# New places for the operations at both ends of a software-pipelined graph-network kernel, written in the order of their places

## Chip, cores and metric

The kernel runs on one core of a Trainium2 chip. The time is device microseconds of one execution; of several runs the median is taken. TensorE (PE) does the matrix products, VectorE (DVE) and ScalarE (ACT) read and write PSUM banks and SBUF, GpSimd (POOL) works on SBUF, and the queue of SyncE (SP) issues the transfers. Each engine runs its own instructions in order and waits on semaphores for the others.

## What is computed

64 graphs of 256 nodes with 512 features pass two layers, all in float32. For each graph:

```python
# layer 0
h   = maximum(layernorm(x), 0)
agg = (adj @ h) / maximum(adj.sum(-1), EPS)
x   = x + relu(concatenate([h, agg]) @ W.T)
# layer 1
h   = maximum(layernorm(x), 0)
Xw  = h @ Wv + bv
e   = leaky_relu(sj[None, :] + si[:, None] + ab, 0.2)   # sj, si: Xw times the halves of aw
T   = adj * exp(e);  T = T / T.sum(-1)
H, Xk = 0, h
for k in range(3):
    H  = H + Xk @ Wk[k] + bk[k]
    Xk = T @ Xk
x   = x + relu(H)
```

## The kernel before

**Products.** The matrix products are written in forms with fewer multiplications (seven products in place of eight for 2 x 2 blocks, and a larger form for x·W in `wide`). Their sums and differences run on DVE, POOL and ACT, and most matmuls take a 128x128 block against a 128x256 block. The matmul line is L459 for all of them. PSUM has eight banks of 128x512.

**Stages.** A graph goes through a list of stages. `loads` fetches x and adj; `prepare` makes the first norm and relu (`norm_relu`, L347), scales the adjacency by the degree (`scaled`, L567), and transposes both; `prepared` ends this; `wide` is h times the weights of layer 0, `layer0` the adjacency times that and the residual (`finish`, L563). `turn1` is the second norm, then four multiplications with sums on DVE (L677) that give sj and si. `transition` builds T: ds (L686) writes sj to DRAM, row (L687) reads it back to all partitions, ACT makes the leaky relu (L692) and the exponential (L695), DVE multiplies by adj and sums (L697), ACT scales (L703). `moved` and `once` form T·h, `inner` the inner hop, `turned1` reads the transposed h back, and `outer` makes the products with Wk that end in the output. Work on a graph is spread over several turns: loads go three graphs ahead, `prepare` and `prepared` one ahead, `moved` to `outer` one behind.

**Transposing.** Most graphs transpose through DRAM: DVE turns blocks (L376), SP writes them (`dh`, `dan`, `dtt`, L380) and reads them back (L386). The first graphs and the last two use PE for some of it instead (`flip_on_pe`: matmul against the identity at L404, copied out at L408 to L410).

**Order.** Nothing in the code's own sequence sets the order on an engine. Every operation is put into a `Plan` (`add`) with its engine, a cost (which the program passes to a `note` that does nothing), and the keys that it reads and writes. Its place is a number: the entry of the table `AT` for its stage and its count in that stage, plus graph number times TURN (38.52), plus a shift for graphs near the end. `emit` sorts each engine's operations by place, and each engine runs that list. Tables named for a stage alone hold for the middle graphs; `_0`, `_1`, `_2` hold for the first three, `_last` and `_late` for graphs 63 and 62, and `first` and `weights` for the loads of the first inputs and the preparation of the weights. `emit` goes round the engines and writes, for each, every operation whose forerunners are written; the framework sets semaphores in that sequence.

**First inputs.** SP's first loads are the halves of graph 0's x, the four parts of W (L787 on), adj of graph 0 and 1, x of graph 1, the halves of Wv and the blocks of Wk. PE transposes the parts of W (L796) and of Wv (L848), and DVE makes the sums of W's form.

**The last product.** `main` (L527) makes the seven products of a 2 x 2 form, numbered by `step`, in PSUM. `p`, `r` and `d` are its three banks; `plus` (L474) adds a known term to the product in bank p and puts it into the bank where a later product is then accumulated: its seed. In the last graph two more banks, x and y, are given, so that each quarter of the output can leave as soon as it is ready (`last`, L756: relu and residual on DVE, then a DMA of the quarter). There the seed for product 3 goes first into the upper half of bank r; after product 2, which accumulates in the lower half of bank r, ACT copies it to bank y (L546), where product 3 accumulates:

```python
plus(bank[r][:, hi], [f"bank{r}"], p, lo, s12, keys[1:])
...
step(2, r, lo, terms)
add("ACT", 0.37, lambda: nc.scalar.copy(bank[y][:, lo], bank[r][:, hi]), [f"bank{r}"], [f"bank{y}"])
last(0, lo, r, lo)
step(3, y, lo, terms)
last(0, hi, y, lo)
```

Of the kernel before, what the change touches and what calls it, by code (L numbers as in the profile page):

```python
# [11 lines left out]
AF = mybir.ActivationFunctionType  # L12
# [15 lines left out]
    "first": (-90.93, -53.23, -117.99, -108.94, -110.36, -116.23, -69.23, -51.75, -160.39, -107.21, -61.21, -22.37, -27.53, -12.34, -45.26, -1.78,  # L28
        -84.29, -28.27, -93.32, 13.37, -47.15, -20.43, -156.60, -71.50, -119.21, -46.84, -42.27, -129.45, -122.63, -61.71, -52.35, -32.94, -72.67,
        -62.56, -45.91, -151.57, -67.52, -60.72, 2.83, 15.02, -11.78, 19.40, 29.16, -47.95, -25.77, 48.23, -47.81, -32.81, -19.46, -48.89, 7.13,  # L30
        20.41, -32.63, 17.85, 10.53, -123.51, 5.76, 21.86),
    "inner": (105.13, 108.59, 106.23, 109.69, 109.89, 110.76, 112.05, 116.38, 111.97, 114.07, 117.47, 117.50, 122.79, 115.08, 117.06, 118.02, 137.51),
    "inner_0": (104.64, 107.10, 112.63, 109.63, 108.85, 109.21, 114.17, 115.99, 113.73, 110.41, 129.80, 114.72, 119.54, 110.75, 113.34, 116.02,
        129.11),
    "inner_1": (110.70, 112.22, 111.49, 112.47, 113.83, 115.31, 114.08, 115.66, 116.33, 115.18, 129.29, 117.74, 125.91, 116.89, 117.80, 117.56,
        155.03),
    "inner_2": (110.70, 111.20, 111.98, 113.63, 111.78, 114.32, 114.94, 116.88, 115.46, 116.06, 116.42, 116.98, 124.86, 117.74, 119.04, 117.57,
        134.35),
    "inner_last": (336.53, 367.29, 384.59, 334.45, 391.73, 454.67, 522.64, 533.37, 408.60, 470.37, 504.02, 528.93, 492.30, 558.54, 500.07, 537.12,
        580.23),  # L40
    "inner_late": (108.31, 111.76, 110.85, 113.85, 112.13, 112.69, 114.05, 114.68, 123.33, 115.61, 145.82, 118.27, 122.89, 115.88, 119.11, 120.04,
        164.89),
    "layer0": (20.96, 24.01, 34.26, 38.15, 36.30, 37.47, 38.90, 39.56, 40.20, 40.90, 41.49, 42.16, 41.93, 42.79, 43.22, 43.47, 44.25),
    "layer0_0": (43.30, 43.73, 40.76, 63.15, 62.04, 64.91, 63.69, 65.17, 65.45, 66.86, 68.03, 68.37, 68.31, 69.19, 69.32, 68.45, 68.75),
    "layer0_1": (31.27, 36.57, 33.97, 43.43, 46.13, 48.74, 46.62, 49.21, 46.86, 49.66, 48.01, 49.83, 48.25, 48.79, 50.67, 49.93, 50.78),
    "layer0_2": (24.88, 28.19, 23.22, 43.47, 37.98, 37.09, 39.47, 39.22, 40.19, 41.59, 40.57, 42.04, 42.75, 43.10, 41.23, 47.00, 44.33),
    "layer0_last": (50.01, 57.68, 33.91, 60.79, 65.66, 66.71, 68.41, 66.94, 69.01, 68.24, 69.91, 69.27, 70.80, 71.03, 72.73, 71.96, 75.23),
    "layer0_late": (15.20, 21.71, 35.30, 40.31, 42.84, 48.47, 47.89, 49.57, 47.98, 49.76, 48.90, 49.94, 48.91, 50.48, 49.70, 51.70, 50.97),
    "loads": (-59.49, -45.29),
    "loads_2": (-40.12, -36.06),  # L50
    "loads_last": (-58.91, -32.90),
    "loads_late": (-54.89, -85.13),
    "moved": (89.04, 92.46, 93.17, 93.66, 94.15, 98.50),
    "moved_0": (94.08, 96.00, 97.15, 96.58),
    "moved_1": (87.63, 93.34, 94.62, 96.56, 97.69, 105.10),
    "moved_2": (88.68, 91.56, 91.23, 91.84, 96.02, 106.19),
    "moved_last": (139.05, 163.46, 205.96, 169.91),
    "moved_late": (96.66, 97.72, 100.63, 101.15),
    "once": (61.25, 64.00, 75.09, 75.88, 94.29, 95.59, 94.96, 99.41, 98.19, 98.63, 100.80, 101.23, 101.56, 100.30, 105.75, 103.00, 102.97, 103.89,
        106.56, 107.35, 108.14),  # L60
    "once_0": (85.34, 86.38, 98.69, 87.50, 93.62, 98.46, 98.58, 97.73, 98.58, 100.34, 100.69, 102.20, 101.36, 98.56, 103.24, 103.33, 102.27, 102.98,
        104.33, 105.25, 108.42),
    "once_1": (57.59, 69.48, 97.24, 96.50, 95.31, 95.58, 95.01, 99.66, 97.26, 98.27, 100.29, 102.15, 100.46, 102.80, 103.34, 105.40, 106.15, 108.95,
        105.21, 110.88, 111.17),
    "once_2": (63.41, 76.25, 69.81, 96.68, 93.52, 97.13, 93.09, 100.30, 100.95, 102.43, 103.05, 103.30, 102.21, 102.90, 103.59, 109.13, 104.57,
        107.39, 107.54, 109.97, 115.46),
    "once_last": (102.80, 135.83, 148.28, 162.89, 124.41, 120.18, 145.98, 187.50, 162.35, 203.89, 212.10, 233.57, 187.89, 213.05, 223.02, 232.11,
        256.18, 243.42, 255.25, 267.18, 321.27),
    "once_late": (66.99, 88.23, 64.29, 90.92, 99.96, 101.37, 100.45, 101.19, 101.37, 101.90, 105.80, 107.13, 110.31, 103.81, 110.60, 107.37, 105.93,
        106.50, 106.70, 107.63, 115.35),  # L70
    "outer": (108.93, 110.52, 122.87, 129.37, 114.22, 117.68, 119.41, 120.07, 120.70, 121.57, 122.87, 123.53, 124.60, 125.46, 126.33, 126.99, 127.62,
        130.65, 131.52, 132.19, 128.92, 131.95, 134.55, 134.99, 141.93, 152.31, 138.02, 140.19, 162.69, 160.60, 164.14, 164.93),
    "outer_0": (94.35, 98.74, 125.62, 106.70, 102.31, 116.27, 117.12, 118.24, 117.50, 117.80, 121.31, 124.46, 124.00, 125.58, 126.52, 126.71, 128.22,
        128.87, 132.65, 133.67, 128.80, 131.21, 134.36, 137.61, 140.55, 144.44, 136.33, 141.49, 160.49, 160.36, 163.66, 166.03),
    "outer_1": (106.89, 111.90, 118.77, 120.53, 108.75, 117.68, 119.18, 119.21, 120.59, 120.95, 123.23, 122.93, 123.75, 126.63, 126.70, 127.43,
        127.87, 128.74, 130.19, 132.33, 130.44, 131.84, 139.05, 141.13, 148.79, 152.10, 133.45, 136.68, 160.29, 160.80, 164.22, 166.72),
    "outer_2": (108.39, 111.96, 127.91, 140.81, 108.40, 121.23, 123.19, 121.63, 124.71, 125.64, 126.27, 125.65, 128.28, 128.68, 129.01, 128.91,
        131.04, 134.92, 135.36, 134.36, 132.23, 135.69, 137.94, 142.17, 143.69, 152.32, 138.41, 140.22, 150.30, 161.80, 164.00, 171.57),
    "outer_last": (498.02, 668.57, 694.33, 671.17, 577.46, 581.61, 593.26, 565.87, 615.19, 623.17, 650.49, 630.60, 695.13, 726.44, 735.87, 784.68,
        743.01, 838.42, 843.34, 796.04, 842.17, 761.60, 792.50, 751.08, 788.70, 811.00, 818.37, 858.45, 840.44, 876.17, 953.80, 975.74, 975.14,  # L80
        1020.56, 876.63, 891.60, 907.44, 875.80, 872.80),
    "outer_late": (109.06, 117.31, 186.73, 151.51, 116.15, 116.30, 119.62, 120.47, 120.01, 120.90, 123.12, 123.38, 129.10, 132.52, 132.66, 129.78,
        134.77, 139.77, 140.44, 139.50, 141.87, 144.49, 145.13, 158.57, 188.07, 200.85, 150.49, 152.04, 158.47, 232.29, 199.18, 211.96),
    "prepare": (-43.06, -41.74, -40.72, -35.30, -36.24, -28.72, -27.19, -23.45, -19.80, -15.93, -24.36, -24.98, -20.94, -12.75, -1.76, -2.28, -14.82,
        -13.49, -12.68, -12.13, -11.03, -11.58, -0.32, 1.04, 0.48, 2.14, 1.59),
    "prepare_0": (-84.88, -53.30, -37.93, -28.72, -22.39, -78.13, -74.85, -6.63, -18.20, -7.49, -144.71, -60.68, -137.04, -101.76, -12.58, -21.22,
        -26.38, -2.11, -10.47, 18.05),
    "prepare_1": (-15.07, -17.62, -8.06, -6.13, -0.14, -1.19, -0.63, 0.54, 7.75, 18.63, -38.44, -18.61, -14.54, 4.73, 16.46, 7.28, 12.55, 17.02,
        21.02, 19.33),
    "prepare_2": (-29.75, -29.48, -28.24, -24.75, -27.62, -28.40, -18.19, -16.40, -14.88, -13.91, -13.33, -6.35, -3.17, 8.62, 7.51, 7.67, -7.58,  # L90
        -2.32, -3.08, -1.25, 10.97, -0.12, 9.45, 9.24, 6.13),
    "prepare_last": (-41.49, -47.42, -40.82, -36.74, -38.40, -39.37, -36.21, -27.41, -24.96, -22.93, -7.95, -5.29, -3.53, 0.52, -2.38, -0.41, -8.95,
        -8.06, 0.10, 9.16, 6.05, -3.83, 2.64, 1.68, 2.00, -1.88, -3.02),
    "prepare_late": (-34.61, -47.32, -24.01, -19.75, -22.44, -22.19, -20.22, -19.93, -12.10, -16.22, -28.31, -35.76, -26.99, -25.62, -0.63, -19.64,
        -11.10, -13.45, -13.43, -9.03, -11.19, -7.53, -0.35, -0.68, -1.43, -1.97, 0.33),
    "prepared": (-7.18, 5.89, 11.28),
    "prepared_0": (8.94, 11.22, 28.01, 44.28),
    "prepared_1": (30.89, 31.47, 31.46, 30.86),
    "prepared_2": (13.00, 25.59),
    "prepared_last": (9.25, 6.90, 2.69),  # L100
    "prepared_late": (-3.13, 0.63, 10.23),
    "transition": (52.39, 56.28, 64.51, 63.42, 65.05, 63.97, 66.52, 67.12, 67.73, 68.04, 68.40, 68.92, 69.51, 71.25, 71.80, 70.70, 72.35),
    "transition_0": (74.09, 74.94, 85.61, 86.74, 87.55, 87.22, 90.49, 90.24, 90.60, 91.41, 91.25, 92.03, 91.61, 91.53, 93.51, 94.10),
# [6 lines left out]
    "turn1_1": (49.63, 49.70, 50.51, 51.10, 51.13, 51.73, 53.03, 53.21, 53.66, 53.93, 58.29, 58.86, 64.81, 54.56, 54.30, 58.29, 62.00, 58.02, 61.54),  # L110
    "turn1_2": (43.11, 45.01, 43.93, 52.82, 53.16, 53.50, 49.16, 51.40, 52.03, 52.20, 54.30, 57.90, 58.08, 51.29, 54.09, 59.58, 56.28, 52.52, 56.97),
    "turn1_last": (75.41, 78.96, 77.17, 178.47, 184.64, 192.21, 86.15, 103.27, 80.59, 81.84, 83.21, 85.38, 104.79, 93.44, 122.16, 115.84, 150.29,
        115.69, 113.30),
    "turn1_late": (42.12, 48.32, 51.63, 53.75, 53.93, 54.07, 55.81, 56.33, 52.09, 61.66, 67.71, 71.29, 74.60, 66.82, 79.34, 84.95, 89.16, 79.81,
        97.48),
    "turned1": (100.59,),
# [859 lines left out]
```

## Time and profile before

| | us |
|---|---|
| median of 3 runs | 2546.91 (2546.01 to 2550.6) |
| profiled execution, its time | 2545.75 |
| its span | 2544.0 |
| PE busy | 2509.1 (99%) |
| DVE, POOL, ACT busy | 1653.6, 1560.1, 1322.6 |
| granted TensorE clock, mean | 0.997 |

The span runs from the first to the last instruction, and the execution's own time is 1.75 us longer. The page's second part shows the span in 40 slices of 63.6 us. The busiest groups are the products of L459, with 380 ns for a matmul alone and 1.03 us for four back to back. A bracket at the end of a row, such as [2.09 <-ACT bank L546], is the idle time of that engine before the row and what ended it.

### The profile page before, as it was taken

The page shows a single profiled execution, that of the slowest core. Times are in us where ns is not written, and L with a number is a line of the kernel's source. Part 1 is how long each engine was busy: PE and PEld are TensorE (multiplying, and loading weights), DVE is VectorE, ACT ScalarE, POOL GpSimd, SP SyncE. Part 2 cuts the span into 40 slices and gives each one's busy share as a digit, 9 for nine tenths or more (in the row PEclk, how much of TensorE's full clock was granted, in tenths as well). Part 3 has the DMA queues.
Part 4 walks back from the last instruction along what each step waited for, and adds up shares of the span by engine and source line. Part 5 has one row for each costly group of instructions (what it writes and reads, how often), then busy time and mean ns, then how long its engine had stood idle before and what let it go on. Part 6 is the DMA issues. An engine that isn't in the chain of part 4 may idle for free.

```text
span 2544.0 us, 39950 instructions
## 1 busy us (share of the span) xinstructions
PE 2509.1 (99%) x12412; PEld 2213.5 (87%) x12412; DVE 1653.6 (65%) x4099; ACT 1322.6 (52%) x3551; POOL 1560.1 (61%) x2475
## 2 busy tenths in 40 slices
PE   7899999999999999999999999999999999999998
PEld 5688888888888888888888888888888888888887
DVE  5766666666666666666666666666666666666654
ACT  7455555555555555555555555555555555555521
POOL 5565666666666666666666656656666666666640
PEclk9999999999999999999999999999999999999999
DMA  4354454454454454444444544544544544544421
GB/s 150 85 131 117 113 129 120 115 125 117 117 129 112 115 135 110 119 125 120 120 120 116 127 121 111 128 122 113 127 119 117 126 113 116 135 112 115 110 71 44
DMA packets 574571, 296.85 MB, mean 117 GB/s; under 512 B 417171, under 2 KB 540819, under 8 KB 574358
## 3 DMA queue, kind: packets, MB, share of 16 engines
q1 hardware_dynamic: 574358, 294.31, 47.0%
q8 instruction: 98, 1.61, 0.3%
q14 instruction: 115, 0.94, 0.1%
HBM read 162.80 MB, written 131.40 MB: 116 GB/s over the span
## 4 chain that ended last, share of the span: by engine, by line
PE 96%; DVE 1%; DMA 1%; SPq 0%; ACT 0%; issue 0%; POOL 0%; DVEq 0%; ACTq 0%; POOLq 0%
PE bank L459 96%; DMA dh<-turned 0%; DMA x<-in_L_gnn_W_dram 0%; DMA l<-in_L_gnn_Wv_dram 0%; SPq L380 0%; DVE bank L474 0%; DVE zg L420 0%; DMA out_dram<-x 0%; DVE z L677 0%; DVE turned L376 0%; PE bank L404 0%; ACT h1n L362 0%; DVE bank L652 0%; SPq L345 0%; DVE zg L474 0%
## 5 line engine op out<-in xcount | busy, mean ns | idle before, releaser
L459 PE MATMUL bank<-l,s 128*128 128x256 f32 x3292 | 876.9, 380 | 6.6 <-ACT bank L546 2.1
L459 PEld LDWEIGHTS bank<-l,s 128*128 128x128 f32 x3292 | 611.6, 191 | 91.4 <-issue 5.1
L471 ACT COPY stg<-bank 128x256 f32<-128x256 f32 x944 | 337.2, 371 | 524.8 <-PE bank L459 203.6
L459 PE MATMUL bank<-l,zg 128*128 128x256 f32 x1820 | 469.2, 380 | 1.6 <-ACT mz L471 0.9
L459 PE MATMUL bank<-lq,zg 128*128 128x256 f32 x1792 | 447.8, 380 | 3.7 <-DVE zg L474 1.3
L459 PEld LDWEIGHTS bank<-lq,zg 128*128 128x128 f32 x1792 | 340.4, 190 | 51.1 <-DVE zg L474 2.3
L459 PEld LDWEIGHTS bank<-l,zg 128*128 128x128 f32 x1820 | 337.2, 191 | 42.3 <-ACT mz L471 1.7
L422 POOL TENSOR_TENSOR zg<-zg 128x256 f32<-128x256 f32 x183 | 131.7, 733 | 353.8 <-ACT zg L471 347.4
L652 DVE TENSOR_TENSOR bank<-bank,stg 128x256 f32<-128x256 f32 x505 | 210.3, 428 | 202.1 <-PE bank L459 138.8
L459 PE MATMUL bank<-l,h0t 128*128 128x256 f32 x1008 | 291.3, 382 | 1.6 <-DVE q L652 0.8
L422 POOL TENSOR_TENSOR s<-h0t,s 128x256 f32<-128x256 f32 x315 | 234.0, 743 | 0.5
L459 PEld LDWEIGHTS bank<-l,h0t 128*128 128x128 f32 x1008 | 197.4, 197 | 26.8 <-DVE q L652 2.3
L677 DVE SCALAR_TENSOR_TENSOR z<-h1n,v_sb 128x512 f32<-128x512 f32 x256 | 211.9, 828 | 13.1 <-ACT h1n L368 4.4
L459 PE MATMUL bank<-l,h1t 128*128 128x256 f32 x784 | 203.3, 381 | 1.3 <-DVE lo L477 1.0
L471 ACT COPY qf<-bank 128x256 f32<-128x256 f32 x128 | 47.6, 372 | 285.3 <-DVE qf L474 250.3
L422 POOL TENSOR_TENSOR qf<-qf 128x256 f32<-128x256 f32 x122 | 113.5, 930 | 117.4 <-DVE qf L474 117.4
L459 PEld LDWEIGHTS bank<-l,h1t 128*128 128x128 f32 x784 | 153.1, 197 | 20.1 <-DVE lo L477 2.3
L563 DVE SCALAR_TENSOR_TENSOR x<-bank,x 128x512 f32<-128x512 f32 x254 | 165.4, 686 | 2.7 <-PE bank L459 1.9
L459 PE MATMUL bank<-q,sa 128*128 128x256 f32 x512 | 152.9, 380 | 2.3 <-DVE bank L474 1.6
L459 PE MATMUL bank<-qf,st 128*128 128x256 f32 x512 | 152.6, 380 | 0.8 <-DVE qf L420 0.7
L422 POOL TENSOR_TENSOR s<-h0t 128x256 f32<-128x256 f32 x189 | 143.5, 773 | 9.3 <-ACT h0t L410 6.6
L422 POOL TENSOR_TENSOR hf<-h1n,hf 128x256 f32<-128x256 f32 x124 | 91.3, 736 | 89.9 <-PE bank L459 89.9
(178 smaller groups left out, 4418.3 us busy)
## 6 DMA issues: line engine op xcount, KB each, us to landing
dh<-turned SPq DMA_DIRECT2D x500, 128.0 KB, 3.3
h1t<-dh SPq DMA_DIRECT2D x64, 512.0 KB, 3.8
x<-in_x_dram SPq DMA_DIRECT2D x63, 512.0 KB, 4.6
out_dram<-x SPq DMA_DIRECT2D x63, 512.0 KB, 3.1
h0t<-dh SPq DMA_DIRECT2D x61, 512.0 KB, 4.0
a<-in_adj_dram SPq DMA_DIRECT2D x64, 256.0 KB, 4.3
dan<-turneda SPq DMA_DIRECT2D x248, 64.0 KB, 1.9
raw<-dan SPq DMA_DIRECT2D x62, 256.0 KB, 2.7
```

The lines of the kernel that those rows point to most:

```text
L422: add("POOL", cost, lambda: getattr(nc.gpsimd, f)(to, p, q), reads, writes)
L459: nc.tensor.matmul(ps, lhs, rhs, start=start, stop=True, skip_group_check=True)
L471: add("ACT", 0.37, lambda: nc.scalar.copy(dst, bank[b][:, cols]), [f"bank{b}"], dkeys)
L563: add("DVE", 0.75 if sums else 0.69, lambda c=c: nc.vector.scalar_tensor_tensor(t[:, c, :], bank[banks[1 + c]], 0.0, t[:, c, :], op0=ALU.m ...
L652: add("DVE", 0.43, lambda f=f, to=to, x=x, y=y: getattr(nc.vector, f)(to, x, y), pbk + [k], tok)
L677: add("DVE", 0.79, lambda s=s, c=c: nc.vector.scalar_tensor_tensor(scr.rearrange("p c n -> p (c n)"), h[:, c, :], 1.0, v_sb[:, s, :], op0= ...
```

## The change

The text of the change has four parts.

1. New numbers in `AT` for `first`, `weights`, and for all tables `_0`, `_1`, `_2`, `_last` and `_late`. Of the tables for the middle graphs only one number of `inner` differs, 117.47 to 117.62. Which operations there are stays the same, apart from part 4.
2. `emit` writes one operation at a time, the one with the lowest place among the engines' next operations that are ready, in place of a run of ready operations for one engine after another.
3. Three of the costs on ACT operations with sums are set higher.
4. In `main`, for the last graph, the seed of product 3 goes to the lower half of its own bank; ACT's copy is left out.

```diff
 AT = {
-    "first": (-90.93, -53.23, -117.99, -108.94, ...
+    "first": (-259.48, -286.32, -474.02, -306.06, ...
...
-    "transition_0": (74.09, 74.94, 85.61, 86.74, 87.55, 87.22, 90.49, ...
+    "transition_0": (61.61, 65.18, 81.16, 82.84, 81.31, 85.36, 81.78, ...
...
@@ emit
-            for e, queue in queues.items():
-                while heads[e] < len(queue) and self.ops[queue[heads[e]]][2] <= done:
-                    i = queue[heads[e]]
-                    self.ops[i][1]()
-                    done.add(i)
-                    heads[e] += 1
-                    left -= 1
+            ready = [(self.ops[q[heads[e]]][3], e) for e, q in queues.items() if heads[e] < len(q) and self.ops[q[heads[e]]][2] <= done]
+            if ready:
+                e = min(ready)[1]
+                i = queues[e][heads[e]]
+                self.ops[i][1]()
+                done.add(i)
+                heads[e] += 1
+                left -= 1
@@ norm_relu
-                add("ACT", 0.66, lambda c=c: nc.scalar.activation(h[:, c, :], s[:, c, :], AF.Identity, ...
+                add("ACT", 0.82, lambda c=c: nc.scalar.activation(h[:, c, :], s[:, c, :], AF.Identity, ...
...
@@ main
         p, r, d = banks[:3]
+        e, cols = (banks[4], lo) if last else (r, hi)
...
-        plus(bank[r][:, hi], [f"bank{r}"], p, lo, s12, keys[1:])
+        plus(bank[e][:, cols], [f"bank{e}"], p, lo, s12, keys[1:])
         step(7, p, lo, terms)
         if last:
-            x, y = banks[3:]
+            x = banks[3]
...
             step(2, r, lo, terms)
-            add("ACT", 0.37, lambda: nc.scalar.copy(bank[y][:, lo], bank[r][:, hi]), [f"bank{r}"], [f"bank{y}"])
             last(0, lo, r, lo)
-            step(3, y, lo, terms)
-            last(0, hi, y, lo)
+            step(3, e, cols, terms)
+            last(0, hi, e, cols)
```

Read off the two built programs, the engines' orders differ in about the first four graphs and the last three; between them each engine has the same instructions in the same order. On SP, the 512 KB of graph 1's x now come first, then the parts of W with the halves of graph 0's x between them, and graph 0's adj after W, which before came second. On PE, one group of four transposes of W and the first two products of graph 0's `wide` stand between and behind the two flips of its h, ahead of the first transposes of Wv. In `transition` of graph 0, ds and row follow one another on SP; on ACT the degree sums of graph 2 stand outside that stage; on DVE the two operations of L697 stand between the additions of graph 1's `layer0`; the two of L703 are neighbours on ACT.

## Prediction

> **What bounds the kernel now.** I began with the page's first two parts and the chain that ended last.
>
> ```profile
> PE 2509.1 (99%) x12412; PEld 2213.5 (87%) x12412; DVE 1653.6 (65%) x4099; ACT 1322.6 (52%) x3551; POOL 1560.1 (61%) x2475
> ...
> PE   7899999999999999999999999999999999999998
> ...
> PEclk9999999999999999999999999999999999999999
> ...
> PE 96%; DVE 1%; DMA 1%; SPq 0%; ACT 0%; issue 0%; POOL 0%; DVEq 0%; ACTq 0%; POOLq 0%
> ```
>
> TensorE does everything that counts. It idles 2544.0 − 2509.1 = 34.9 us in the whole span, and the slices put this into the first and last of them. The change keeps TensorE's number of instructions and, from graph 3 to graph 61, every engine's order. So only the ends are at stake, and I cut them into windows (columns: length, PE, PEld, DVE, ACT and POOL busy, granted clock, DMA share, GB/s).
>
> ```profile
> 0.00:20.00 20.00, 9.95 (x45) 8.29 (x46) 7.35 (x23) 12.97 (x37) 3.13 (x14) 1.00 0.95 314
> 20.00:40.00 20.00, 19.90 (x84) 12.42 (x83) 13.26 (x25) 16.37 (x44) 15.39 (x19) 0.92 0.50 160
> 40.00:60.00 20.00, 17.54 (x85) 12.53 (x85) 13.78 (x36) 13.79 (x39) 11.84 (x18) 1.00 0.01 1
> 60.00:80.00 20.00, 14.65 (x59) 9.89 (x57) 14.15 (x35) 13.05 (x38) 15.70 (x25) 0.95 0.33 60
> 80.00:100.00 20.00, 15.23 (x66) 11.79 (x65) 14.34 (x38) 9.10 (x25) 9.74 (x13) 0.80 0.48 112
> 100.00:120.00 20.00, 18.07 (x81) 14.60 (x80) 13.56 (x28) 6.98 (x22) 11.27 (x18) 1.00 0.34 80
> 120.00:140.00 20.00, 20.00 (x108) 18.09 (x107) 14.04 (x38) 12.03 (x33) 9.99 (x17) 1.00 0.53 125
> ```
>
> Length less PE busy is the idle time: 10.05, 0.10, 2.46, 5.35, 4.77, 1.93 and 0.00. So 24.7 of the 34.9 us are lost before 120 us, 14.6 of them after the first 20. Busy time hides a second loss: the clock is halved in three stretches, 19.9 to 23.35, 77.96 to 88.20 and 2535.55 to 2538.97. In the second PE is busy 6.52 us at clock 0.50, which costs 3.3 more; in the first and the third, 3.4 us each, 1.7. The time at stake is thus 24.7 + 5.0 at the start, and at the end 2.1 + 1.7 (below).
>
> **The parts of the change, one by one.**
>
> *Writing in order of place.* Each engine's queue is sorted as before; only the sequence in which the queues are written differs. It adds no instruction. Where two engines only read one bank, it can turn round which of them waits. In the steady part no engine's order changes: 0. The three cost notes are not used in the program: 0.
>
> *First 24 us: loads and weights.* SP now issues graph 1's 512 KB of x before W, and graph 0's 256 KB of adj after W. The transfers land in order of issue: the four 512 KB parts of W at 4.2, 7.1, 9.0 and 11.0, with 256 KB of adj or x ahead of each but the first, which from 7 us on is about 1.35 us for 512 KB and 0.7 for 256. PE starts on W's first pair at 7.14. With x1 and x0 instead of adj ahead of it I estimate 7.1 + 1.3 = 8.4, and for the second pair, with 256 KB more ahead, 11.7 instead of 11.0: +0.7 at the point where PE has both. In return four transposes of W and two first products of graph 0's `wide` now stand between and behind the flips of its h, ahead of the first transposes of Wv. They fill the waits from 15.4 to 19.6 us, which in the trace are 0.23, 0.79 and the 1.22 for Wv: −2.2. Net **−1.5**. If the half clock behind them stays away too, −3.2; if the loads are late and nothing is filled, +0.7.
>
> *24 to 115 us: graph 0's chain.* The stalls are those of one chain through graph 0: turn1, transition, flip on PE, once, inner. The rows around it:
>
> ```profile
> 57.78 0.35 SPq L686 DMA_DIRECT2D ds<-sj  x1
> 63.50 0.35 SPq L380 DMA_DIRECT2D dh<-turned  x1
> 63.94 0.44 SPq L687 DMA_DIRECT2D row<-ds  x1
> ```
>
> ds had landed at 61.8, but its reader stands behind a dh write that waited for data: 2.1 us of hold. The row lands at 67.3 and ACT comes to it at 68.77, after two scalings of graph 2's adjacency: 1.5.
>
> ```profile
> 69.86 0.72 ACT L695 ACTIVATE z<-z 128x256 f32<-128x256 f32 x2
> ...
> 76.99 0.49 ACT L703 ACTIVATE an<-z,tot 128x256 f32<-128x256 f32 x1
> 77.65 1.52 ACT L368 ACTIVATE h1n<-x,nmr,rstd 128x512 f32<-128x512 f32 x2 [0.17 <-POOL nmr L366]
> 79.08 0.49 ACT L703 ACTIVATE an<-z,tot 128x256 f32<-128x256 f32 x1
> ```
>
> The exponentials end at 70.6, yet their first reader on DVE (L697) runs at 74.41, since it stands behind graph 1's two finishing operations (73.16 and 73.79), which wait for PE: 3.8. The second half of the scaled transition follows the first by 2.1 us instead of 0.5, because a norm of graph 1 lies between: 1.6. After the change ds and row are issued one behind the other, graph 2's adjacency no longer lies on ACT between them, L697 stands between the additions of graph 1's layer0, and the two L703 are neighbours. What SP moves back for it, the dh writes of graph 0's normed rows, is written from 63.50 to 74.4 and read back only at 81.64 (SP's rows), so the slip of some us finds 7 us of room. So the first flip can come 2.1 + 1.5 + 3.8 = 7.4 us earlier (77.5 → about 70), and the second 9.0. PE sees it here:
>
> ```profile
> 77.53 0.44 PE L404 MATMUL bank<-ident,an 128*128 128x128 f32 x2 [0.74 <-ACT an L703]
> 79.62 0.69 PE L404 MATMUL bank<-ident,an 128*128 128x128 f32 x2 [1.65 <-ACT an L703]
> ...
> 85.31 1.19 PE L459 MATMUL bank<-l,s 128*128 128x256 f32 x2 [1.61 <-ACT stg L471]
> ```
>
> Not all of it becomes time: PE's queue is in order, and graph 1's layer0 and graph 2's product stand around the flip. At stake are 14.6 of idle and 3.3 of half clock, 17.9. I went through the new order by hand, every operation at the duration of its row (pair of 128x256 products 0.51 to 0.59, ACT copy 0.37, DVE sum 0.42, POOL sum 0.74, a write and a read back through DRAM 5 to 7): PE has the work that it had done at 115 us done 17.8 us earlier, 1.8 of them from the first part, 16.0 from this one. The walk gives each hand-over nothing (the trace has 0.05 to 0.1), doesn't see POOL and DVE queue for each other, and each of these puts some of the stalls back one step later: late next are graph 0's two products of once (94.00, behind DVE) and h0t of graph 3 from SP (issued 100.34). I take two thirds of the 17.9: **−11.5**, about 4 of it before 75 us. Ends: −16.0 (the walk) and 0 (graph 0 is bound by its DRAM round trips and another wait takes each place).
>
> POOL gets no additional operations. DVE and ACT carry the same work in less time; at 14 of 20 us busy DVE is the fullest, and this is why I don't take the walk.
>
> *The last product.* Before, product 3's seed lay in the upper half of the bank that product 2 writes, and ACT copied it out (L546):
>
> ```profile
> 2532.44 0.76 DVE L474 TENSOR_TENSOR bank<-bank,lo 128x256 f32<-128x256 f32 x2 [4.74 <-PE bank L459]
> 2533.24 0.75 DVE L756 SCALAR_TENSOR_TENSOR x<-bank,x 128x256 f32<-128x256 f32 x2
> ...
> 2534.08 0.36 ACT L546 COPY bank<-bank 128x256 f32<-128x256 f32 x1 [13.70 <-DVE x L756]
> 2534.49 1.13 PE L459 MATMUL bank<-l,s 128*128 128x256 f32 x4 [2.09 <-ACT bank L546]
> 2535.46 1.82 PE L459 MATMUL bank<-l,h1t 128*128 128x256 f32 x4
> ```
>
> PE waits 2.09 us for a copy that itself sits behind DVE's two output operations on the same bank. After the change DVE writes the seed directly into its own bank, product 3 long has it, and PE's new order puts products with 2.2 us of work after product 7, more than the 1.2 that DVE needs for the two seeds. The stall goes: −2.1. What is late next is DVE's last output and the DMA, as before. Two rows before and one after show what the stall brings along: four products take 1.82 us instead of 1.03, and this lasts 3.4 us: −1.7. The Trainium skill, "TensorE: Matmul & The Clock Gate", section "HAM oscillation — how this bites in real kernels", has "no PE-idle gaps >~3.4µs" as the rule; by it a gap of 2.09 would not bring the half clock, it would be there for other reasons and stay: −2.1 alone. The trace shows full clock and no gap over 1 us in the 5 us before it; I take the row, **−3.8**. The same page, section "Part 1: The HAM clock gate (the "warmup" mystery)", says the window runs freely and that the place of the change differs from run to run. This speaks against counting on the clock at the start, hence the two thirds.
>
> *Other places of the last two graphs.* The last graph's other stalls, 0.8, 0.85, 0.84 and 0.85, keep their causes. Graph 62's outer loses a cover (+0.45), the last layer0 gains one (−0.5): 0, ends −2 and +2, the 3 us that graph 62 stalls now.
>
> **Sum**: −1.5 − 11.5 − 3.8 = −16.8 from the profiled execution's 2545.75 gives 2528.95. The median of the three runs lies 1.16 above the profiled one, so 2530.1: **2530 us**.
>
> **Rivals.** *A. Full walk*: start −17.8, end −3.8: 2525; speaks for it that the holds are plainly other work in line; against, a full DVE. *B. Half the start*, −6.5, and the end: 2537. *C. Only the end*: 2543; for it, 7.4 us of holds are less than the round trips of the chain (57.8 to 67.3 for ds and row alone), against it, those 7.4 are visible. *D. Slower*: ACT is in order, and its Prelu (L692) on the row now stands earlier, in front of the copies that free PE's banks. Before, the row was there 1.5 us before ACT was. If in the first graphs SP or the v products are late and the row isn't there, ACT stands, and PE runs dry behind it: 3 to 5 us in each of three graphs, +9 to +15 with the end's −3.8, some 2553. It decides as soon as the row lands over 4 us after ACT has come to it. *E. It doesn't do what it says*: if the writing order alone is in force, no order of an engine changes and the time is 2547; but the orders do differ in the first four graphs.
>
> **Numbers.** Measured differences below 0.2% (5.1 us) can't be told from none. Chances: forecast (2526 to 2534) 0.40, A 0.20, B 0.20, C 0.10, D 0.07, E 0.03. The range 2520 to 2542 leaves out D, E and half of C at the top, and a walk with the clock's gain and the late graphs' −2 at the bottom. Faster (below 2541.8): the forecast, A, B and some of C, 0.87; same 0.06, slower 0.07.
>
> **What would show it.** In the changed kernel's windows: idle before 120 us near 13 instead of 24.7, clock 1.00 from 60 to 100; the first flip of graph 0 near 70 us, ds and row issued within 5 us, L697 within 1 us of the exponentials; no L546, no gap over 1 us in the last 12 us of PE, clock 1.00 there. I am wrong if PE's idle moves to 100 to 140 us, if ACT idles on row for more than 2 us, or if half clock turns up in new places.

## The result, and the profile after

| | before | after |
|---|---|---|
| median of 6 runs, us | 2548.26 (2546.01 to 2550.6) | 2535.84 (2534.51 to 2536.98) |
| ratio, 95% interval | | 0.9951 [0.9939, 0.9964] |
| profiled execution: time, span, us | 2545.75, 2544.0 | 2535.3, 2533.5 |
| PE busy, idle within the span, us | 2509.1, 34.9 | 2501.0, 32.5 |

The change makes the kernel 12.4 us faster by the medians and 10.5 by the two profiled executions, where 16.8 were forecast; 2530 was predicted, with 2520 to 2542 as the range. Here is the windows view of the changed kernel, with the columns as before (length, PE, PEld, DVE, ACT, POOL busy, granted clock, DMA share, GB/s).

```profile
0.00:20.00 20.00, 7.31 (x39) 6.28 (x40) 6.10 (x20) 10.81 (x30) 2.04 (x11) 0.95 0.91 330
20.00:40.00 20.00, 19.69 (x84) 11.85 (x83) 11.05 (x26) 16.14 (x47) 14.64 (x20) 0.88 0.45 131
40.00:60.00 20.00, 19.08 (x93) 14.53 (x93) 14.27 (x38) 14.99 (x41) 12.31 (x18) 1.00 0.01 1
60.00:80.00 20.00, 15.62 (x68) 10.89 (x67) 16.72 (x47) 15.54 (x47) 14.97 (x25) 1.00 0.29 57
80.00:100.00 20.00, 17.32 (x86) 13.87 (x85) 14.56 (x42) 10.75 (x32) 12.36 (x16) 1.00 0.73 172
100.00:120.00 20.00, 18.05 (x81) 14.89 (x81) 12.08 (x30) 8.09 (x23) 9.97 (x18) 1.00 0.33 77
120.00:140.00 20.00, 20.00 (x106) 18.04 (x107) 11.99 (x32) 11.22 (x31) 16.45 (x24) 1.00 0.57 138
```

PE's idle time fell by only 2.4 us and its busy time by 8.1: most of what was gained is time in which PE counts as busy and its matmuls are slow, not gaps. Three things stand out in the windows. The half clock from 78 to 88 us is gone (1.00 from 40 us on), though the one at the start now lasts from 17.9 to 24.7 us instead of 19.9 to 23.3. The idle time from 20 to 120 us fell from 14.6 to 10.2 us. But the first 20 us idle 12.7 instead of 10.05, and the clock from 20 to 40 is 0.88 instead of 0.92: at the start, where 1.5 us had been forecast as a gain, the windows show none.

Windows of equal time hold unequal work, so I used a second account. The 6256 products and transposes that PE has to do need 2483.3 us at full clock (0.433 us for a product of 128x128 by 128x256, 0.108 for a transposed block, as in the rows of the middle). At each point in this work, the time at which the trace shows it done, less the work so far, is what PE has lost: idle, half clock and slow first matmuls together. PE's order is different at the ends, but the work done is comparable. The losses in us at five points, for all kernels of this study:

| kernel | 10 us of work | 30 | 110 (about 150 us) | 2360 | 2474 | end |
|---|---|---|---|---|---|---|
| before | 17.35 | 20.04 | 43.46 | 43.88 | 52.65 | 57.52 |
| after | 18.61 | 21.22 | 36.61 | 36.19 | 46.04 | 46.86 |
| 1 seed alone | 18.01 | 20.70 | 43.94 | 44.04 | 52.81 | 53.64 |
| 2 new start alone | 15.99 | 18.60 | 32.82 | 54.20 | 63.86 | 64.69 |
| 3 new ends and seed | 18.91 | 21.60 | 44.79 | 46.56 | 56.45 | 57.28 |
| 4 new writing alone | 18.27 | 20.96 | 42.87 | 64.51 | 73.28 | 74.11 |
| 5 writing and one number | 17.28 | 19.97 | 41.70 | 42.42 | 50.39 | 51.22 |
| 6 after, flips moved | 19.61 | 22.22 | 37.35 | 37.48 | 47.34 | 48.16 |
| 7 after, x1 later | 18.90 | 21.51 | 36.48 | 36.39 | 46.16 | 46.99 |
| 8 after, old ends | 18.04 | 20.65 | 35.75 | 36.16 | 44.12 | 44.95 |
| 9 after, old ends, mixed writing to 0 | 16.86 | 19.46 | 34.43 | 33.67 | 41.64 | 42.46 |
| 10 the same, to 160 | 16.95 | 19.56 | 33.88 | 33.41 | 41.38 | 42.20 |
| 11 as 5, and the seed | 18.56 | 21.25 | 42.61 | 43.16 | 51.12 | 51.94 |
| 12 after, again | 18.58 | 21.19 | 36.06 | 35.67 | 45.51 | 46.34 |

Of the 10.66 us between before and after at the end, 7.7 were gained up to 2360 us of work and 4.05 behind 2474 (4.87 lost there before, 0.82 after), and 1.1 were given back between. The scatter can be read from kernels that are alike up to a point: before, 1 and 3 have the same start and differ by up to 1.6 us at 10 and 30 us of work; after, 8 and 12 by up to 0.6. From 30 us of work to 110, and from 2360 on where their ends are the same, kernels alike agree within 0.6. From 110 to 2360 us the scatter is larger: experiment 3 loses 1.8 us there, the kernel before 0.4 and experiment 1 0.1, with the same middle graphs.

### The profile page after: what moved, and what is told of

It reads as the page before. It is cut to its first block, busy times and chain, and to the rows that moved or that the text cites. A ratio compares the mean times of both kernels' runs of the same rounds, so it can differ in the third digit from the quotient of the medians.

```text
span 2533.5 us, 39965 instructions
## 1 busy us (share of the span) xinstructions
PE 2501.0 (99%) x12412; PEld 2206.4 (87%) x12412; DVE 1646.6 (65%) x4099; ACT 1323.1 (52%) x3550; POOL 1561.3 (62%) x2475
## 4 chain that ended last, share of the span: by engine, by line
PE 96%; DVE 1%; POOL 1%; DMA 1%; ACT 1%; issue 0%; SPq 0%; DVEq 0%; POOLq 0%; ACTq 0%
PE bank L461 96%; DMA raw<-dtt 0%; DMA x<-in_x_dram 0%; DMA raw<-dan 0%; POOL s L424 0%; DMA dtt<-turneda 0%; PE bank L406 0%; ACT h1n L364 0%; ACT h1n L370 0%; POOL rstd L367 0%; POOL sa L424 0%; DVE bank L476 0%; POOL q L424 0%; DVE bank L654 0%; POOL l L777 0%
## 5 line engine op out<-in xcount | busy, mean ns | idle before, releaser
L424 POOL TENSOR_TENSOR s<-h0t 128x256 f32<-128x256 f32 x189 | 143.0, 772 | 14.9 <-ACT h0t L412 12.4
```

The source lines that it names most:

```text
L424: add("POOL", cost, lambda: getattr(nc.gpsimd, f)(to, p, q), reads, writes)
```

## Experiments 1 to 4: the parts alone

**Seed alone.** The kernel before with part 4 of the change; the copy's place is taken out of the list.

```diff
+        e, cols = (banks[4], lo) if last else (r, hi)
...
-        plus(bank[r][:, hi], [f"bank{r}"], p, lo, s12, keys[1:])
+        plus(bank[e][:, cols], [f"bank{e}"], p, lo, s12, keys[1:])
...
-            add("ACT", 0.37, lambda: nc.scalar.copy(bank[y][:, lo], bank[r][:, hi]), [f"bank{r}"], [f"bank{y}"])
...
-            step(3, y, lo, terms)
-            last(0, hi, y, lo)
+            step(3, e, cols, terms)
+            last(0, hi, e, cols)
```

> Kernel before with part 4 of the change alone: product 3's seed goes by DVE into its own bank in the last graph, ACT's copy is left out, no other place moved. If the stall of 2.09 us is what halves the clock behind it (the rows), PE's end comes 3.8 us earlier than in the kernel before, with full clock to the end; if the half clock has another cause (the rule on idle gaps), 2.1 us earlier and the clock stays halved for about 3.4 us. If DVE's two output operations hold the seed back as they held the copy, a stall of 1 to 2 us stays in the old place and less than 1 us is gained.

Measured: 2543.29 against 2546.6 us, ratio 0.9987 [0.9981, 0.9994]; loss after 2474 us of work 0.83 instead of 4.87 us, so 4.0 gained. PE's rows at the end of this kernel:

```profile
2531.97 0.59 PE L466 MATMUL bank<-qf,st 128*128 128x256 f32 x2
2532.40 1.03 PE L466 MATMUL bank<-l,s 128*128 128x256 f32 x4
2533.26 1.03 PE L466 MATMUL bank<-l,h1t 128*128 128x256 f32 x4
2534.12 1.03 PE L466 MATMUL bank<-l,zg 128*128 128x256 f32 x4
```

In the kernel before, the last of these groups was:

```profile
2537.07 1.91 PE L459 MATMUL bank<-l,zg 128*128 128x256 f32 x4
```

The four matmuls of l,s follow without a gap, and the next two groups take 1.03 us, where before they took 1.82 and 1.91. PE's order is the same; the stall was taken away and the half clock went with it. The row was right, and the rule of the Trainium skill ("TensorE: Matmul & The Clock Gate", "HAM oscillation — how this bites in real kernels", gaps over 3.4 us) was too wide for this place: a gap of 2.09 us was enough.

**New start alone**, with the old writing: new numbers for `first`, `weights` and the first three graphs.

```diff
-    "first": (-90.93, -53.23, -117.99, ...
+    "first": (-259.48, -286.32, -474.02, ...
...
-    "transition_2": (50.97, 58.93, 62.74, ...
+    "transition_2": (52.17, 57.73, 65.68, ...
```

> Kernel before with the new places of the first inputs, the weights and the first three graphs, and nothing else. If the parts of the change simply add, PE stands 7 to 8 us earlier from graph 4 to the end (what the profile of the changed kernel shows at 150 us), its waits before 24 us are the same as in the changed kernel (4.1 us for the copy of h0t), and the time is 7 to 8 us under the one before. If the writing in order of place is needed for the gain (other waits at the readers of one bank), 3 us or less.

Measured: 2556.81 us, ratio 1.004 [1.0026, 1.0054]: slower by 0.4%. Neither theory holds. Up to 110 us of work this kernel gains 10.6 us on the one before, 3.8 more than the changed kernel; its wait before the first product is 2.69 instead of 4.08 us, and the clock from 20 to 40 us is 1.00. But then it loses 21.4 us in the middle graphs, whose places are the old ones and where each engine has its old order.

**New ends and seed**: new numbers for graphs 62 and 63.

```diff
-    "outer_late": (109.06, 117.31, 186.73, ...
+    "outer_late": (194.61, 225.39, 317.02, ...
...
-    "outer_last": (498.02, 668.57, 694.33, ...
+    "outer_last": (1243.02, 1439.80, 1512.86, ...
```

> Kernel before with the new places of the last two graphs and the seed in its own bank. By the profile of the changed kernel the new places of graph 62 lose 1.4 us and the last product gains 4.0, so 2.6 us under the kernel before, and 1.2 us more than the seed alone leaves. The rival, that the places of the last two graphs are neutral as predicted and the 1.4 us were given back because the start came earlier: 3.8 to 4.0 us under the kernel before, like the seed alone.

Measured: 2544.49 us, ratio 0.9993 [0.9985, 1.0001], by the time alone unclear. In the account it loses 9.89 us from 2360 to 2474 us of work, the kernel before 8.77 and the seed alone 8.77. So the new places lose 1.1 us in the last graphs without a new start as well; the first theory had 1.4.

**New writing alone**: `emit` as in the change, all places old.

```diff
-            for e, queue in queues.items():
-                while heads[e] < len(queue) and self.ops[queue[heads[e]]][2] <= done:
+            ready = [(self.ops[q[heads[e]]][3], e) for e, q in queues.items() if heads[e] < len(q) and self.ops[q[heads[e]]][2] <= done]
+            if ready:
+                e = min(ready)[1]
```

> Kernel before with the writing in order of place alone. No engine's order changes, so the time stays within 1 us and the windows up to 140 us show the same idle times (24.7 us in all). The rival: which reader of a bank waits for which is turned round, and some waits in the first 120 us move by 1 us or more, to either side.

Measured: 2562.34 us, ratio 1.0062 [1.005, 1.0075]: 15.7 us slower, against both expectations. The start and the end are no worse (from 2474 on 0.83 us are lost); the loss lies in the middle, 21.6 us from 110 to 2360 us of work, which is 0.37 for each of some 58 graphs. The windows of the middle, first of the kernel before:

```profile
400.00:1200.00 800.00, 800.00 (x3989) 712.92 (x3988) 526.48 (x1309) 426.54 (x1144) 508.94 (x810) 1.00 0.49 120
```

and of the writing alone:

```profile
400.00:1200.00 800.00, 797.36 (x3953) 705.14 (x3952) 520.91 (x1296) 422.20 (x1132) 503.49 (x800) 1.00 0.49 120
```

PE did 36 matmuls less in the same 800 us, which at 0.2165 us each are 7.8 us, with only 2.64 us of idle time to show for it. The two programs differ, within a middle graph, in one pair of waits. ACT's copy t3 and DVE's sum t2, operations 10 and 11 of `inner`, both read the lower half of one bank. The timeline of the kernel before at such a place, DVE and then ACT:

```profile
1035.59 0.42 DVE L474 TENSOR_TENSOR qf<-bank,qf 128x256 f32<-128x256 f32 x1 [0.18 <-PE bank L459]
1035.95 0.43 DVE L474 TENSOR_TENSOR bank<-bank,p 128x256 f32<-128x256 f32 x1
```

```profile
1036.05 0.37 ACT L471 COPY qf<-bank 128x256 f32<-128x256 f32 x1 [4.26 <-DVE qf L474]
```

With the writing alone, ACT, DVE and PE:

```profile
1003.82 0.37 ACT L479 COPY qf<-bank 128x256 f32<-128x256 f32 x1 [3.73 <-PE bank L467]
```

```profile
1004.29 0.42 DVE L482 TENSOR_TENSOR qf<-bank,qf 128x256 f32<-128x256 f32 x1 [0.58 <-ACT qf L479]
1004.63 0.42 DVE L482 TENSOR_TENSOR bank<-bank,p 128x256 f32<-128x256 f32 x1
```

```profile
1004.05 1.03 PE L467 MATMUL bank<-l,zg 128*128 128x256 f32 x4
1005.20 0.67 PE L467 MATMUL bank<-q,sa 128*128 128x256 f32 x2
```

PE's rows at this place in the kernel before:

```profile
1035.75 1.03 PE L459 MATMUL bank<-l,zg 128*128 128x256 f32 x4
1036.62 0.59 PE L459 MATMUL bank<-q,sa 128*128 128x256 f32 x2
```

Before, DVE reads as soon as PE is done and ACT, which is in no hurry, waits for DVE. Now ACT reads first, DVE waits 0.58 for ACT, and the next DVE operation, the seed in layer0 on which PE stands, comes later: PE starts q,sa 1.15 us after l,zg, where it was 0.87 before. The 0.36 us of such a place can be read from these rows: 0.12 is idle time; 0.16 is lost because the first matmul of q,sa no longer starts before the last one of l,zg has ended (0.87 against 1.03), which counts as busy; and 0.08 because q,sa takes 0.67 instead of 0.59. Nearly all of PE's idle time in the middle lies at this place, 6.4 us from 400 to 2400 us with the writing alone:

```profile
L467 PE MATMUL bank<-q,sa 128*128 128x256 f32 x408 | 125.2, 388 | 6.4
```

That two readers wait for each other at all agrees with the Trainium skill, "PSUM — Partial Sum Buffer", section "PSUM bank collisions raise a hardware error": accesses of two engines to one bank must be kept apart, reads included. Which of them waits was decided here by which is written first (experiments 4 and 5). By place ACT's copy comes first (117.47 against 117.50). The old `emit` writes a run of DVE operations before it comes to ACT, and in the kernel before that turned out well in every middle graph; in experiment 2 the same `emit`, come to the middle from another start, turned out badly in all of them. DVE's waits from 200 to 2200 us (52 graphs) for this sum show it, first before, then with the writing alone, then in experiment 2 (us in total, times, longest):

```profile
DVE qf L474 <- PE bank L459: 9.2, 52, 0.2
DVE qf L482 <- ACT qf L479: 30.0, 51, 0.9
DVE qf L482 <- ACT qf L479: 30.6, 52, 0.9
```

So the one new number in the middle tables, 117.47 to 117.62, which the prediction passed over, may be what the new writing needs: it puts ACT's copy behind 117.50. Experiment 5 tries it.

## Experiments 5 to 8: the pair, the start, the ends

**Writing and the one number.**

```diff
-    "inner": (..., 114.07, 117.47, 117.50, ...
+    "inner": (..., 114.07, 117.62, 117.50, ...
```

> Kernel before with the writing in order of place and, besides, the one new number of the middle graphs, 117.62 for operation 10 of inner; all other places old. In the run with the writing alone PE lost 0.35 us in every middle graph, and there DVE's sum t2 (operation 11, place 117.50) waits for ACT's copy t3 (operation 10, place 117.47) of the same bank; in the kernel before ACT waits for DVE. If this one pair is the whole of it, the new number turns the wait back, no loss is left between 150 and 2360 us, and the time is within 1.5 us of the kernel before. If the writing order costs in other places too, some of the 16 us stay.

Measured: 2541.77 against 2547.68 us, ratio 0.9978 [0.9971, 0.9985]. The middle loses nothing (41.70 at 110, 42.42 at 2360): within the scatter the pair is the whole of the 21.6 us. But the time is 5.9 us under the kernel before, where it had been expected within 1.5. Up to 110 us of work 1.8 of this is gained, about the scatter; 4.8 come after 2360, and 4.0 of these in the last 10 us, in which the seed is still copied. Its rows, ACT and then PE:

```profile
2528.93 0.36 ACT L554 COPY bank<-bank 128x256 f32<-128x256 f32 x1 [12.07 <-PE bank L467]
```

```profile
2529.55 0.59 PE L467 MATMUL bank<-qf,st 128*128 128x256 f32 x2
2529.98 1.03 PE L467 MATMUL bank<-l,s 128*128 128x256 f32 x4
2530.84 1.03 PE L467 MATMUL bank<-l,h1t 128*128 128x256 f32 x4
```

The copy waits for PE alone, because it is now written ahead of DVE's output operation on the same bank, and has long ended when product 3 starts. What stalled the last product was not the copy itself but another pair of readers turned the wrong way.

**Flips moved.** In the changed kernel, three places of graph 0's `prepare`: copy of the first flip, second flip, its copy.

```diff
-    "prepare_0": (..., -107.43, -80.74, -221.81, -184.46, -141.15, -88.95),
+    "prepare_0": (..., -107.43, -80.74, -221.81, -280.00, -200.00, -183.00),
```

> Changed kernel with three places of graph 0's prepare moved: ACT's copy of the first flip straight behind the flip (ahead of a copy for the sums of W), the second flip ahead of the first two products, its copy seven operations earlier on ACT. If the wait of 4.08 us before PE's first product is due to the copy's place, the product starts at 17.1 to 17.3 us, when DVE has its weights, instead of 18.66, POOL's first sum comes 3 to 4 us earlier, and PE is 1.4 to 3 us ahead of the changed kernel at 115 us; less half clock if the gap is what halves it. The rival, that DVE's chain of sums for W bounds the start anyway: less than 0.5 us.

Measured: 2537.99 us, ratio 0.9963 [0.995, 0.9976], 0.7 to 1.3 us above the two executions of the changed kernel at 110 us of work. The first product did start at 17.48, but only two matmuls long; 1.03 for ACT and 1.89 us for DVE's weights follow before 23.2. The rival holds: once ACT carries the flip's copy early, its copies for the sums of W come 0.3 us later, and DVE's chain of these sums is what ends next.

**x1 later.** In the changed kernel, the place of the load of graph 1's x behind W:

```diff
-    "first": (..., -203.45, -533.74, -116.49),
+    "first": (..., -203.45, -205.00, -116.49),
```

> Changed kernel with graph 1's x loaded behind W and graph 0's x instead of first. If the 512 KB ahead of W delay the whole start, as the prediction had it (1.3 us), W, x and all that follows come 1.3 us earlier and PE is 1.0 to 1.4 us ahead at 25 us. The rival: ACT and DVE bound the start from 13 us on, the copy of h0t stays late behind them, and PE is less than 0.4 us ahead.

Measured: 2535.64 us, ratio 0.9957 [0.9942, 0.9972]; loss at 30 us of work 21.51 against 21.22 and 21.19 of the changed kernel. PE's wait before the first product is 4.08 as there. The number is the rival's, but the run doesn't settle what the load of x1 costs: ACT now waits for graph 0's adjacency, which it read at 11.77 without a wait in the changed kernel.

```profile
12.88 0.42 ACT L579 ACTIVATE an<-a 128x256 f32<-128x256 f32 x1 [1.40 <-DMA a<-in_adj_dram]
```

What the earlier W may gain is lost there; the first product starts at 19.31 instead of 18.66.

**Old ends.** The changed kernel with the old numbers for graphs 62 and 63.

```diff
-    "outer_late": (194.61, 225.39, 317.02, ...
+    "outer_late": (109.06, 117.31, 186.73, ...
```

> Changed kernel with the old places of the last two graphs, the seed still in its own bank. By the comparison of the runs with the seed alone and with the new places at the end, the new places lose 1.8 us between 2360 and 2520 us whatever stands before them: 1.8 us less than the changed kernel, and the last 10 us as in it. The rival, that the old places suit only the old start: no gain.

Measured: 2533.39 us, ratio 0.9948 [0.9932, 0.9965]. From 2360 to the end it loses 8.79 us, the changed kernel 10.67 in both executions: 1.9 us, as expected. The new places of the last two graphs make the kernel slower.

## Experiments 9 to 12: the pairs at the start

At the start, the run with the new start and old writing and the changed kernel have the same order on each engine and differ in three pairs of readers of W's transposed parts. Here is ACT in the changed kernel:

```profile
14.97 0.37 ACT L473 COPY q<-bank 128x256 f32<-128x256 f32 x1 [0.87 <-DVE q L816]
15.24 0.81 ACT L370 ACTIVATE h0n<-x,nmr,rstd 128x512 f32<-128x512 f32 x1
16.83 0.37 ACT L473 COPY zg<-bank 128x256 f32<-128x256 f32 x1 [0.78 <-DVE l L816]
...
17.98 0.63 ACT L412 COPY h0t<-bank 128x512 f32<-128x512 f32 x1
```

```profile
18.66 2.07 PE L461 MATMUL bank<-l,h0t 128*128 128x256 f32 x4 [4.08 <-ACT h0t L412]
```

Twice ACT waits for a DVE operation that only reads the same bank, 0.87 and 0.78, and behind stands the copy of h0t for which PE waits 4.08. **Mixed writing** takes this away: operations with a place below 0 are written as in the kernel before, the rest in order of place; the ends are the old ones.

```diff
             before = left
+            for e, queue in queues.items():
+                while heads[e] < len(queue) and self.ops[queue[heads[e]]][3] < 0 and self.ops[queue[heads[e]]][2] <= done:
+                    i = queue[heads[e]]
+                    self.ops[i][1]()
+                    done.add(i)
+                    heads[e] += 1
+                    left -= 1
+            if left < before:
+                continue
             ready = [(self.ops[q[heads[e]]][3], e) for e, q in queues.items() if heads[e] < len(q) and self.ops[q[heads[e]]][2] <= done]
```

> Changed kernel with two parts turned back: the places of the last two graphs are the old ones (as in the run before), and operations with a place under 0 (graph 0's norm, the sums of W, the first products) are written engine by engine as in the kernel before, the rest in order of place. No engine's order in the first graphs differs from the changed kernel; only three pairs of readers of one bank wait the other way round, ACT's copies of W's parts no longer for DVE. If these pairs made the wait of 4.08 us before the first product, that wait is 2.7 us as in the run with the new start and old writing, PE is 2.4 to 3.3 us ahead of the changed kernel at 30 us (the half clock may or may not come) and keeps it, the middle loses nothing, and the time is 4.5 to 5.5 us under the changed kernel. The rival, that the difference between these runs at the start is chance of transfers and clock: as the run with the old places at the end, 1.9 us under the changed kernel.

> As the run with places under 0 written engine by engine, but up to place 160, so that five more pairs in once and inner of graphs 0 and 1 also wait as under the old writing. In the run with the new start and old writing PE gained 0.5 to 1.2 us more on the changed kernel between 60 and 110 us. If these pairs are the cause, 0.5 to 1.2 us less than the run with places under 0; if not, the same within 0.5 us.

> The changed kernel itself once more, on the chip of the mixed runs, so that these can be compared with it. The wait before the first product is 4.0 to 4.2 us again, and PE's end less its work at 30 us lies within 1 us of the first profile of it (21.2 us); if the start is largely chance, further off than that.

Measured, on one chip: 2530.46 us (2529.57 to 2531.51) with mixed writing to place 0, ratio to before 0.9935 [0.9923, 0.9948]; 2530.56 (2529.81 to 2532.97) with it to place 160; the changed kernel again 2534.92 (2534.85 to 2535.47). ACT and PE with mixed writing to 0:

```profile
13.98 0.36 ACT L489 COPY q<-bank 128x256 f32<-128x256 f32 x1
14.23 0.82 ACT L386 ACTIVATE h0n<-x,nmr,rstd 128x512 f32<-128x512 f32 x1
14.95 0.36 ACT L489 COPY zg<-bank 128x256 f32<-128x256 f32 x1
...
16.08 0.64 ACT L428 COPY h0t<-bank 128x512 f32<-128x512 f32 x1
```

```profile
17.25 1.91 PE L477 MATMUL bank<-l,h0t 128*128 128x256 f32 x4 [2.69 <-DVE l L832]
```

The copy of h0t comes 1.9 us earlier, and PE's wait is 2.69 as in experiment 2, now for DVE. At 30 us of work the lead on the two executions of the changed kernel is 1.7 to 1.8 us, less than the 2.4 expected; the half clock stays in part (0.97 from 20 to 40 us, 0.88 and 0.89 in the changed kernel, 1.00 in experiment 2). It is kept to the end, with the 1.9 of the old ends: 4.5 us by the medians, the lower edge of what was expected. **This kernel beats both.** The pairs up to place 160 bring 0.55 us at 110 us of work and nothing in the time: not settled. The changed kernel's wait was 3.49 in its second profile, not 4.0 to 4.2 as expected, since the transpositions before it ended later; but the product starts within 0.25 us of the first profile, and the loss at 30 is within 0.1 of it. The start is not chance.

**Writing, the number, and the seed**, on the kernel before:

> Kernel before with writing in order of place, 117.62 for operation 10 of inner, and now the seed in its own bank as well. Without the seed part, the last stall of 2.09 us had already gone, because ACT's copy was written ahead of DVE's output operation on the same bank and no longer waits for it. If so, the seed in its own bank adds nothing once the writing is changed: the same as without it within 0.5 us by PE's end less its work, no half clock in the last 10 us in either. The rival, that the copy still costs a hand-over: 0.4 to 0.8 us less than without the seed part.

Measured: 2540.84 us, ratio 0.9977 [0.9968, 0.9986], without the seed 0.9978. From 2474 on the loss is 0.82 in this kernel and 0.83 without the seed. With the new writing the seed in its own bank adds nothing; with the old it was worth 4.0 (experiment 1).

## Why the prediction was right, and where not

The direction, the range and the place (the ends) were right. The time lies 5.8 us above the forecast, near the rival with half of the start (2537), and two steps that the sum held at nothing were large and cancelled: that this part came out right is luck, not reasoning.

- *"In the steady part no engine's order changes: 0."* The step failed. The order doesn't change, but the waits do: one pair of readers in each middle graph, 15.7 us slower alone. The one new number in `inner` turns it back. The prediction had said that the writing can turn round which reader waits, and then asked only whether an engine's order changes. The rival "if the writing order alone is in force, the time is 2547" fails with it: it is 2562.
- *First 24 us, −1.5.* It didn't come: at 30 us of work before, 1 and 3, with the old start, have lost 20.0 to 21.6, and the changed kernel twice and 8, with the new one, 20.7 to 21.2. The two products were put where the waits had been, but they waited 4.08 us for ACT's copy, and ACT for DVE, at pairs turned by the writing. With the same places and these pairs not turned, experiment 2 has lost 18.6 there and experiments 9 and 10 19.5, less than every kernel with the old start and writing: the places were worth about what was forecast, and the writing took it away. The 0.7 for the load of x1 didn't show either: PE starts on the last of W at the same time, before and after.

```profile
11.08 4.32 PE L796 MATMUL bank<-ident,x 128*128 128x128 f32 x19 [1.12 <-DMA x<-in_L_gnn_W_dram]
11.07 1.86 PE L798 MATMUL bank<-ident,x 128*128 128x128 f32 x15 [0.17 <-DMA x<-in_L_gnn_W_dram]
```

- *Graph 0's chain, −11.5.* Mis-sized: from 30 to 110 us of work the kernel before lost 23.4 us, the changed one 15.4, so −8.0; the kernels alike to each of them give the same within 0.6. Of what was at stake the half clock, 3.3, went wholly: from 60 to 100 us all kernels with the old start show it and none with the new. Of the 14.6 us of idle time only 4.4 went, and here the term was too large. (Two thirds of 17.9 are 11.9, not 11.5; that changes little.) Here are rows of SP, ACT and PE in the changed kernel:

```profile
60.74 0.34 SPq L689 DMA_DIRECT2D row<-ds  x1
```

```profile
66.49 0.37 ACT L473 COPY stg<-bank 128x256 f32<-128x256 f32 x1 [1.25 <-PE bank L461]
66.76 0.53 ACT L694 ACTIVATE z<-row,si 128x256 f32<-128x256 f32 x1
...
71.82 0.91 ACT L705 ACTIVATE an<-z,tot 128x256 f32<-128x256 f32 x2 [2.28 <-DVE tot L702]
```

```profile
73.22 0.38 PE L406 MATMUL bank<-ident,an 128*128 128x128 f32 x2
```

  The row is issued 3.2 us earlier, but takes 4.3 us to land where it took 3.4 before, and is there at 65.0. ACT comes to it at 66.76, because it stands behind a copy that waits 1.25 us for PE. So ACT's hold on the row is 1.7 us against 1.5 before: graph 2's adjacency is gone from there, and another hold took its place. ACT scales 5.2 us earlier (71.82 against 76.99), and the first flip follows at 73.22, 4.3 us earlier instead of 7.4, since PE's queue has products ahead of it. The guess of two thirds was nearer than the walk, and still too high.
- *The last product, −3.8.* Measured −4.05, stall and half clock both gone, as the row had it and not the rule: the largest gap of PE's last 12 us is 0.62, at clock 1.00. The cause was named rightly (the copy stands behind DVE's operations on its bank); that the seed's own bank is what frees it holds for experiment 1 only. In the changed kernel the writing would have done it alone, as experiments 5 and 11 let expect.
- *Places of the last two graphs, 0, ends −2 and +2.* Measured +1.1 with the old writing and +1.9 with the new, near the upper end.
- *Slower, by ACT standing on the row.* It didn't occur; ACT was late and not the row.
- *Signs.* Clock 1.00 from 60 to 100 us, ds and row within 5 us (2.7) came, and so did the three signs of the end. L697 runs 0.7 and 1.1 us behind the exponentials. PE's idle time before 120 us is 22.9 us, not near 13, and the first flip is at 73.22, not near 70.

What is shown: the pair in `inner` (4 against 5), the pairs at the start (2 and 9 against the changed kernel), the ends (3 and 8), the tail (1, 5, 11). Only argued: why the chain of graph 0 gained 8 and not 11.5; the copy that holds ACT was read from the trace and not tried. The turned pair in experiment 2's middle graphs was read from its waits, too; the one new number was not tried with the old writing.

## What to carry to other kernels

Where engines run fixed orders, the orders don't tell the waits: two engines that read one PSUM bank were put one behind the other here, and the sequence in which the program is written decided who waits. Compare the waits of two programs, not only their orders, and let the reader that stands before the bottleneck be written first. A number that seems to have slipped into a change may be what holds it up; try each part alone, also those that "do nothing".

## What was not expected of the hardware

A gap of 2.09 us in PE's work was enough for 3.4 us of half clock, and without this gap the half clock was gone (experiments 1 and 5). At the start a gap of 2.69 us, ahead of the same product, was followed by half clock from 17.7 to 21.1 us in experiment 9 and by none in experiment 2 (clock 1.00 from 0 to 40 us). So the length of one gap doesn't decide it; what does stays open. The stretches of half clock within PE's work, in all traces here, are 3.4, 6.8 or 10.2 us long, whole multiples of 3.4. A wait of 0.58 us on DVE, at a bank that another engine only reads, cost PE 0.37 us in every graph, of which only a third shows as PE's idle time.
